# Layer 3 attention: four heads' outputs on quarters of the columns, softmax sums by GpSimd and a product with ones

## The chip, the cores and the metric

The kernel runs on one core of one Trainium2 chip. The metric is the device time of one execution in microseconds (us), smaller is better. All arithmetic is in float32. The engines are TensorE (PE in the profile; PEld is its weight load), VectorE (DVE), ScalarE (ACT), GpSimd (POOL) and SyncE (SP, which here only issues DMAs). Each works through its own list of instructions in order.

## What is computed

The whole network has four layers: a selective scan over an image, a deformable convolution, a linear-attention transformer with a mixture of experts, and a causal attention with a second mixture of experts. The change is in the attention of layer 3. It works on 4 images of 2304 tokens and 128 channels, with 4 heads of 32 channels:

```python
qkv = jnp.einsum('btc,oc->bto', x, qkv_w) + qkv_b
q, k, v = (heads(t) for t in jnp.split(qkv, 3, axis=-1))
att = jnp.einsum('bhqd,bhkd->bhqk', q, k) * scale
att = jnp.where(causal, att, -jnp.inf)
att = jax.nn.softmax(att, axis=-1)
out = jnp.einsum('bhqk,bhkd->bhqd', att, v)
return jnp.einsum('btc,oc->bto', out, out_w) + out_b
```

`x` is the layer-normed token array, and the result is added to the tokens. The experts of layer 3 follow.

## The kernel before

The function `_layer3` holds the attention. An image is cut into 6 blocks of 384 queries (`BLK`), numbered `j` = 0 to 5, and into 18 key tiles of 128 (`NT`). Block `j` needs its first 3(j+1) key tiles, since the attention is causal. The heads are taken as two pairs (`p` = 0, 1), two heads `r` in a pair. A unit is one key tile `t` of one pair of one block: 4 x 2 x 63 = 504 units in all.

A unit has two halves. `scores` forms, with one product per head on 64 of the rows each, the transposed scores in `scT` (128 keys x 2 heads x 384 queries, two PSUM banks, one buffer), lets ScalarE take exp of them into `pT` in SBUF (five buffers), and on the three key tiles of the diagonal lets GpSimd zero what is masked (`affine_select`). In the last two of these tiles only 256 or 128 queries are computed. `weighed` multiplies `pT` with the values and adds up over the key tiles in the PSUM bank `out`, three units later (`UNIT_LAG`). The tile `values` holds, next to a head's 32 value channels, 32 columns of ones, so that a head's product has 64 columns: 32 outputs and 32 copies of the softmax sum. Two heads fill 128 columns. At the end of a pair ScalarE copies `out` to `raw`, and four DMAs on SP's queue sort the outputs of the four heads into one tile and the sums into another. `divide` inverts the sums in two pieces (`invert`, VectorE), multiplies, and `output` projects the result and adds it to the tokens `T`.

For a stable softmax each query's maximum is subtracted. `largest` works it out one block ahead: `part` forms the scores of 128 queries against up to 512 keys in `sc` (four PSUM banks, one buffer), VectorE adds the causal mask on a row's last part (`later`) and reduces to the maxima (`mx`, `top`), whose negatives go into `spread`. At the end of a block `take` transposes `spread` (TensorE) and adds it into `q` (VectorE), for either pair. There are 5, 7, 9, 12 and 14 parts for blocks 1 to 5, and 3 for block 0.

`prepare` makes `q`, `k` and `v` of a block: `norm` (VectorE, `xn`), `turn` (GpSimd adds the output bias to `T`; TensorE transposes), four projections and `value`. `normed` computes mean and variance of an image (VectorE), and GpSimd a power of it. The transposes, projections, `take` and `output` share one PSUM bank (`ps`, one buffer).

The order on every engine is written out by hand (`manual_schedule`). For each block and pair the main loop runs over its key tiles: `scores`, then parts of the next block's maxima at an even pace, then one step of `divide` if any waits (two empty steps come first, and one between `invert` and `output`), then in every second unit one step of the preparation of the next image (`others`), then `weighed` of the unit three back.

Of the kernel before, what the change touches and what calls it, by code (L numbers as in the profile page):

```python
# [15 lines left out]
F32 = mybir.dt.float32  # L16
# [1892 lines left out]


KW = 512
UNIT_LAG = 3


def _layer3(ctx, env, io, T):

# [63 lines left out]
    def prepare(im, j):  # L1980

        at = bass.ts(j, BLK)
        t = {}

        def norm():
            t["xn"] = sp.tile([P, G3, C], F32, name="xn")
            for g in range(G3):
                i = j * G3 + g
                nc.vector.tensor_scalar(
                    t["xn"][:, g, :],  # L1990
                    im.T[:, i, :],
                    im.mv[:, i, 0:1],
                    im.rstd[:, i : i + 1],
                    op0=ALU.subtract,
                    op1=ALU.mult,
                )

        def turn():

            own = im.T[:, j * G3 : (j + 1) * G3, :]  # L2000
            nc.gpsimd.tensor_add(own, own, bias.to_broadcast([P, G3, C]))
            pt = psum(P, BLK)
            for g in range(G3):
                nc.tensor.transpose(pt[:, bass.ts(g, P)], t["xn"][:, g, :], ident)
            t["xT"] = sp.tile([P, BLK], F32, name="xT")
            nc.scalar.copy(t["xT"], pt)

        def project(s, p):
            pq = psum(P, BLK)
            nc.tensor.matmul(pq, w_qk[:, s, p, :], t["xT"], start=True, stop=True)  # L2010
            if s:
                nc.scalar.activation(
                    im.k[:, p, at], pq, AF.Identity, bias=b_qk[:, s, p : p + 1]
                )
            else:
                nc.vector.tensor_scalar(
                    im.q[:, p, at],
                    pq,
                    b_qk[:, s, p : p + 1],
                    DH3**-0.5,  # L2020
                    op0=ALU.add,
                    op1=ALU.mult,
                )

        def value():
            pv = psum(P, G3, C)
            for g in range(G3):
                nc.tensor.matmul(
                    pv[:, g, :], t["xT"][:, bass.ts(g, P)], w_v, start=True, stop=True
                )  # L2030
            nc.scalar.copy(
                im.v[:, j * G3 : (j + 1) * G3, :, :DH3],
                pv.rearrange("p g (h d) -> p g h d", d=DH3),
            )
# [63 lines left out]
    class Block:  # L2098


        def __init__(self, im, j, p):
            self.im, self.j, self.p = im, j, p
            self.last = (j + 1) * G3 - 1

    def scores(x, t):
        g0 = max(t - x.j * G3, 0)
        cols = slice(g0 * P, BLK)
        sc = pb.tile([P, 2, 512], F32, name="scT")
        for r in range(2):
            rows = slice(r * 64, r * 64 + 64)  # L2110
            nc.tensor.matmul(  # L2111
                sc[:, r, cols],
                x.im.k[rows, x.p, bass.ts(t, P)],
                x.im.q[rows, x.p, x.j * BLK + g0 * P : (x.j + 1) * BLK],
                start=True,
                stop=True,
            )
        pT = sp.tile([P, 2, BLK], F32, name="pT", bufs=UNIT_LAG + 2)
        nc.scalar.activation(pT[:, :, cols], sc[:, :, cols], AF.Exp)  # L2119
        if t >= x.j * G3:  # L2120
            own = pT[:, :, g0 * P : (g0 + 1) * P]
            nc.gpsimd.affine_select(
                out=own,
                in_=own,
                pattern=[[0, 2], [1, P]],
                compare_op=ALU.is_ge,
                fill=0.0,
                base=0,
                channel_multiplier=-1,
            )  # L2130
        x.__dict__.setdefault("pT", {})[t] = pT

    def weighed(x, t):
        g0 = max(t - x.j * G3, 0)
        cols = slice(g0 * P, BLK)
        if t == 0:
            x.out = po.tile([P, BLK], F32, name="out")
        pT = x.pT.pop(t)
        for r in range(2):
            nc.tensor.matmul(  # L2140
                x.out[r * 64 : r * 64 + 64, cols],
                x.im.v[:, t, 2 * x.p + r, :],
                pT[:, r, cols],
                start=t == 0,
                stop=t == x.last,
            )
        if t == x.last:

            raw = sp.tile([P, BLK], F32, name="raw")
            nc.scalar.copy(raw, x.out)  # L2150
            if x.p == 0:
                x.im.sums = [sp.tile([P, BLK], F32, name=f"sums{i}") for i in range(2)]
            for r in range(2):
                for i in range(2):
                    ch, at = (2 * x.p + r) * DH3, r * 64 + i * DH3
# [4 lines left out]
    def divide(x):  # L2160
        oT, den = x.im.sums

        def invert(i):
            part = bass.ts(i, BLK // 2)
            nc.vector.reciprocal(den[:, part], den[:, part])
            if i:
                nc.vector.tensor_mul(oT, oT, den)

        wait = lambda: None
        return [  # L2170
            wait,
            wait,
            lambda: invert(0),
            lambda: invert(1),
            wait,
            output(x.im, x.j, oT),
        ]

    for s in spread:
        nc.gpsimd.memset(s, 0.0)  # L2180
    for v in values:
        nc.gpsimd.memset(v, 1.0)
    images = [Image(b) for b in range(NB)]
    blocks = [Block(im, j, p) for im in images for j in range(NBLK) for p in range(NP3)]

    def preparation(im):
        return normed(im) + [s for j in range(NBLK) for s in prepare(im, j)]

    def run(steps):
        for s in steps:  # L2190
            s()

    with tc.manual_schedule(engines=ORDERED):
# [10 lines left out]
        waiting, done, doing = [], [], []  # L2204
        for i, x in enumerate(blocks):
            n = x.last + 1
            if x.j == 0 and x.p == 0 and x.im.b + 1 < NB:
                others += preparation(images[x.im.b + 1])
            following = blocks[i + NP3] if i + NP3 < len(blocks) else None
            if x.p == 0:  # L2210
                parts, take = largest(following.im, following.j) if following else ([], None)
                total, units = len(parts), 0
                if following and following.im is x.im and x.im.b == 0:

                    need = (NBLK - 1 - following.j) * (2 + 2 * NP3 + 1)
                    need += 0 if x.im.b + 1 == NB else len(preparation(images[1]))
                    while len(others) > need:
                        others.pop(0)()
            for t in range(n):
                scores(x, t)  # L2220
                units += 1
                while parts and (total - len(parts)) * (NP3 * n - 1) < total * units:
                    parts.pop(0)()
                if doing:
                    doing.pop(0)()
                if others and (t % 2 == 0 or n < 7):
                    others.pop(0)()
# [6 lines left out]
            if x.p == NP3 - 1:  # L2234
                run(parts)
                if following and following.im is not x.im:
                    run(others)
                    others = []
                if take:
                    take()  # L2240
        for y, s in waiting:
            weighed(y, s)
            if s == y.last and y.p == NP3 - 1:
                doing += divide(y)
        run(doing)

# [158 lines left out]
```

## Time and profile before

| | us |
|---|---|
| median of 3 runs | 12411.82 |
| lowest and highest run | 12407.96, 12424.98 |
| the profiled execution | 12295.53 |
| its span, first to last instruction | 12293.8 |
| layer 3: first `sc` product to last addition to `T` | 10797.5 to 12090.1 |

| engine | busy in the span |
|---|---|
| TensorE | 10700.3 (87%) |
| weight loads | 8228.4 (67%) |
| VectorE | 8434.0 (69%) |
| ScalarE | 6893.9 (56%) |
| GpSimd | 4463.2 (36%) |

The mean granted TensorE clock was 0.956 of full speed. Busy times are averages over four unlike layers, so a change in layer 3 has to be read in layer 3's stretch of the trace. The profiled execution was 116.3 us shorter than the median of the timed ones. A matmul's recorded end is modelled, and the weight loads of TensorE overlap its products, so starts are surer than durations. A float32 product appears as two MATMUL and two LDWEIGHTS records.

### The profile page before, as it was taken

What the parts mean: (1) busy time and instruction counts of PE and PEld (TensorE: products, weight loads), DVE (VectorE), ACT (ScalarE), POOL (GpSimd) and SP (SyncE); (2) the same over time, 40 slices, a digit from 0 to 9 for tenths busy, and PEclk for the clock granted to TensorE, in tenths of its full rate; (3) what the DMA queues carried; (4) which work ended last, traced back from release to release, by engine and by line L of the source; (5) the groups of instructions that cost most, each with busy time, mean ns of one, the idle gap of its engine ahead of it and who ended that gap; (6) DMA issues with size and microseconds to landing.
All of it is one profiled execution on the core that took longest, in us unless ns stands there. A gap on an engine that the chain in (4) does not pass through costs nothing.

```text
span 12293.8 us, 192110 instructions
## 1 busy us (share of the span) xinstructions
PE 10700.3 (87%) x71008; PEld 8228.4 (67%) x71008; DVE 8434.0 (69%) x15140; ACT 6893.9 (56%) x13190; POOL 4463.2 (36%) x4799
## 2 busy tenths in 40 slices
PE   7778788977888787789979999999999999689997
PEld 6667666766676666578857777777777777433333
DVE  6998889888888889755455655655665665455553
ACT  5777777777777777611135555655565565323332
POOL 2443334333333434377733333333333333110001
PEclk9999999999999999999979999999999999889998
DMA  3221222222212222266600000000000000300003
GB/s 123 69 71 64 76 80 69 65 75 83 67 66 72 69 80 68 80 182 198 195 31 2 4 2 4 5 2 4 2 4 3 3 1 1 126 8 8 8 9 129
DMA packets 329875, 677.47 MB, mean 55 GB/s; under 512 B 41556, under 2 KB 152168, under 8 KB 328048
## 3 DMA queue, kind: packets, MB, share of 16 engines
q1 hardware_dynamic: 276064, 493.50, 12.6%
q0 software_dynamic: 51840, 169.91, 4.9%
q8 instruction: 569, 9.32, 0.3%
q14 instruction: 362, 2.97, 0.1%
q10 hardware_dynamic: 1040, 1.77, 0.0%
HBM read 602.63 MB, written 71.85 MB: 55 GB/s over the span
## 4 chain that ended last, share of the span: by engine, by line
PE 37%; DVE 6%; ACT 4%; DMA 3%; POOL 3%; issue 3%; SPq 0%; ACTq 0%; DVEq 0%; POOLq 0%
PE psum L1466 4%; PE psum L1458 4%; PE pc L1352 3%; PE psum L1402 3%; PE scT L2111 3%; PE psum L1372 2%; POOL g L990 2%; PE psum L1212 2%; DMA g<-table,idx 2%; PE psum L1213 2%; PE psum L1146 2%; PE out L2140 2%; PE sc L2055 2%; PE psum L1290 1%; ACT pT L2119 1%
## 5 line engine op out<-in xcount | busy, mean ns | idle before, releaser
L576 ACT ACTIVATE hs<-ps,bct 128x256 f32<-128x256 f32 x4608 | 1857.5, 475 | 1172.6 <-PE ps L570 1122.1
L570 PE MATMUL ps<-ident,h 128*128 128x128 f32 x9216 | 1492.4, 294 | 786.5 <-DVE h L556 612.3
L570 PEld LDWEIGHTS ps<-ident,h 128*128 128x128 f32 x9216 | 1080.4, 148 | 1170.8 <-DVE h L556 719.5
L584 PE MATMUL yp<-ident,hs 128*128 128x128 f32 x9216 | 1400.4, 288 | 28.6 <-ACT ys L599 28.6
L516 ACT ACTIVATE dA<-delta,l_Al 128x768 f32<-128x768 f32 x1536 | 1388.3, 936 | 0.3
L523 POOL TENSOR_TENSOR h<-du,rB 128x512 f32<-128x512 f32 x768 | 1079.4, 1405 | 766.0 <-PE ps L570 689.5
L584 PEld LDWEIGHTS yp<-ident,hs 128*128 128x128 f32 x9216 | 1154.2, 150 | 82.7 <-ACT ys L599 57.7
L556 DVE TENSOR_TENSOR_SCAN h<-dA,h 128x256 f32<-128x256 f32 (+1 forms) x1024 | 1082.6, 1057 | 27.2
L556 DVE TENSOR_TENSOR_SCAN h<-dA,carry,h 128x768 f32<-128x768 f32 x512 | 1028.7, 2009 | 10.6 <-ACT dA L516 10.6
L1206 POOL TENSOR_TENSOR T<-T,bias 128x384 f32<-128x384 f32 x384 | 384.1, 1000 | 1560.5 <-DVE fn L1134 1520.3
L498 POOL TENSOR_SCALAR_AFFINE_SELECT dB<-bct 128x512 f32<-128x512 f32 x768 | 750.4, 977 | 355.4 <-PE b L530 238.7
L556 DVE TENSOR_TENSOR_SCAN h<-dA,carry,b 128x512 f32<-128x512 f32 x512 | 645.4, 1261 | 267.3 <-PE b L530 247.9
L530 PE MATMUL b<-dB,duT 128*128 128x128 f32 x6144 | 826.9, 278 | 0.8 <-ACT duT L456 0.8
L990 POOL DMA_INDIRECT g<-table,idx x648 | 705.1, 1088 | 242.1 <-issue 139.7
L2119 ACT ACTIVATE pT<-scT 128x768 f32<-128x768 f32 (+2 forms) x504 | 378.1, 750 | 724.9 <-PE scT L2111 724.9
L530 PEld LDWEIGHTS b<-dB,duT 128*128 128x128 f32 x6144 | 766.6, 196 | 2.4 <-POOL h L523 1.2
L1003 PE MATMUL pt<-ident,gw 128*128 128x128 f32 x5184 | 661.7, 283 | 98.9 <-DVE gw L997 94.7
L563 POOL COPY carry<-h 128x2 f32<-128x2 f32 x512 | 97.8, 191 | 1780.9 <-DVE h L556 1722.4
L997 DVE TENSOR_TENSOR gw<-g,wq 128x512 f32<-128x512 f32 x648 | 446.0, 694 | 422.8 <-DMA g<-table,idx 366.0
L1003 PEld LDWEIGHTS pt<-ident,gw 128*128 128x128 f32 x5184 | 608.7, 193 | 146.8 <-DVE gw L997 113.4
L527 DVE TENSOR_TENSOR h<-du,rB 128x512 f32<-128x512 f32 x768 | 628.2, 818 | 2.7 <-DMA rB<-rows 2.5
L1219 ACT ACTIVATE wksq<-psum,l_cols 128x384 f32<-128x384 f32 x192 | 111.6, 581 | 788.3 <-DVE wk L1217 788.3
(394 smaller groups left out, 22793.0 us busy)
## 6 DMA issues: line engine op xcount, KB each, us to landing
rB<-rows SPq DMA_DIRECT2D x768, 384.0 KB, 3.4
w<-f_w SPq DMA_DIRECT2D x64, 1024.0 KB, 12.1
table<-zero SPq DMA_DIRECT2D x162, 128.0 KB, 1.9
table<-tok SPq DMA_DIRECT2D x16, 1152.0 KB, 9.7
g<-table,idx POOLq DMA_INDIRECT x648, 3.8
yd<-y SPq DMA_DIRECT2D x4, 2304.0 KB
sums<-raw SPq DMA_DIRECT2D x192, 48.0 KB, 2.0
xb<-x SPq DMA_DIRECT2D x42, 192.0 KB, 3.4
```

Of the source, the lines that this page charges most:

```text
L498: nc.gpsimd.affine_select(out=x.dB[n], in_=x.bc[:, m0 : m0 + CT // P, n : n + 1].to_broadcast([P, CT // P, P]), pattern=[[0, CT // P], [1, ...
L516: nc.scalar.activation(dA, x.delta[:, d, :], AF.Exp, scale=A[:, d, x.k, n : n + 1])
L523: nc.gpsimd.tensor_mul(h[:, 1, own], x.du[:, 1, own], x.rB[n][:, own])
L527: nc.vector.tensor_mul(x.h[n][:, :, own], x.du[:, :, own], b)
L530: nc.tensor.matmul(b0[:, bass.ts(m, P)], x.duT[:, m, :], x.dB[n][:, m, :], start=True, stop=True,)
L556: nc.vector.tensor_tensor_scan(h, da, b, initial=first, op0=ALU.mult, op1=ALU.add)
L570: nc.tensor.transpose(tt[:, m, bass.ts(d, P)], x.h[n][:, d, bass.ts(2 * q + m, P)], ident)
L576: nc.scalar.activation(hs, tt[:, m, :], AF.Copy, scale=x.bc[:, 2 * q + m, NS + n : NS + n + 1])
L584: nc.tensor.matmul(yp[:, q, (2 * d + m) * P : (2 * d + m + 1) * P], hs[:, bass.ts(d, P)], ident, is_transpose=True, start=n == 0 and m == ...
L990: nc.gpsimd.indirect_dma_start(out=g, out_offset=None, in_=table, in_offset=bass.IndirectOffsetOnAxis(ap=idx[:, j : j + 1], axis=0),)
L1003: nc.tensor.matmul(pt[:, t - t0, :], gw[:, q, :], ident, start=q == 0, stop=q == 3)
L2119: nc.scalar.activation(pT[:, :, cols], sc[:, :, cols], AF.Exp)
```

## The change

A block is no longer split into pairs. A step of the loop is one key tile for both pairs: `scores` of pair 0, `weighed` of the key tile two back (`UNIT_LAG` 2), `scores` of pair 1, then parts, two steps of `divide` and one of `others`. `values` loses its ones, and `weighed` now issues four products, each of a head's 32 value columns on a quarter of the array's columns, into `out`. The softmax sums are made in another way: for each unit GpSimd adds `pT` into a tile `sums` (a copy on the first key tile), and at the end of a block four products with a tile of ones add `sums` over the partitions (the step `sums` of `divide`), which ScalarE copies to `den`. The copy to `raw` becomes one to `oT`, and the DMAs go away. There are eight `pT` buffers. The cut marks leave out lines that stay the same.

```diff
-UNIT_LAG = 3
+UNIT_LAG = 2
...
-    values = [cp.tile([P, NT, NH3, 2 * DH3], F32, name=f"v{i}") for i in range(2)]
+    values = [cp.tile([P, NT, C], F32, name=f"v{i}") for i in range(2)]
+    ones = cp.tile([P, DH3], F32, name="ones")
...
-        pT = sp.tile([P, 2, BLK], F32, name="pT", bufs=UNIT_LAG + 2)
+        pT = sp.tile([P, 2, BLK], F32, name="pT", bufs=2 * (UNIT_LAG + 2))
...
+        if t == 0 and p == 0:
+            x.sums = sp.tile([P, NP3, 2, BLK], F32, name="sums")
+        total = x.sums[:, p, :, cols]
+        if t == 0:
+            nc.gpsimd.tensor_copy(total, pT[:, :, cols])
+        else:
+            nc.gpsimd.tensor_add(total, total, pT[:, :, cols])
+        x.pT[t, p] = pT
 
     def weighed(x, t):
...
-        pT = x.pT.pop(t)
-        for r in range(2):
-            nc.tensor.matmul(
-                x.out[r * 64 : r * 64 + 64, cols],
-                x.im.v[:, t, 2 * x.p + r, :],
-                pT[:, r, cols],
-                start=t == 0,
-                stop=t == x.last,
-            )
+        for p in range(NP3):
+            pT = x.pT.pop((t, p))
+            for r in range(2):
+                ch = slice((2 * p + r) * DH3, (2 * p + r + 1) * DH3)
+                nc.tensor.matmul(
+                    x.out[ch, cols],
+                    x.im.v[:, t, ch],
+                    pT[:, r, cols],
+                    start=t == 0,
+                    stop=t == x.last,
+                )
         if t == x.last:
-            raw = sp.tile([P, BLK], F32, name="raw")
-            nc.scalar.copy(raw, x.out)
...
-                    nc.sync.dma_start(
-                        x.im.sums[i][ch : ch + DH3, :], raw[at : at + DH3, :]
+            x.oT = sp.tile([P, BLK], F32, name="oT")
+            nc.scalar.copy(x.oT, x.out)
+
+    def divide(x):
+        t = {}
+        def sums():
+            pd = psum(P, BLK)
+            for p in range(NP3):
+                for r in range(2):
+                    h = 2 * p + r
+                    nc.tensor.matmul(
+                        pd[h * DH3 : (h + 1) * DH3, :],
+                        ones,
+                        x.sums[:, p, r, :],
+                        start=True,
+                        stop=True,
                     )
+            t["den"] = sp.tile([P, BLK], F32, name="den")
+            nc.scalar.copy(t["den"], pd)
...
         return [
             wait,
-            wait,
+            sums,
             lambda: invert(0),
             lambda: invert(1),
             wait,
-            output(x.im, x.j, oT),
+            output(x.im, x.j, x.oT),
         ]
...
             for t in range(n):
-                scores(x, t)
-                units += 1
-                while parts and (total - len(parts)) * (NP3 * n - 1) < total * units:
-                    parts.pop(0)()
-                if doing:
-                    doing.pop(0)()
-                if others and (t % 2 == 0 or n < 7):
-                    others.pop(0)()
-                waiting.append((x, t))
-                if len(waiting) > UNIT_LAG:
+                scores(x, t, 0)
+                if len(waiting) == UNIT_LAG:
                     y, s = waiting.pop(0)
                     weighed(y, s)
-                    if s == y.last and y.p == NP3 - 1:
+                    if s == y.last:
                         doing += divide(y)
+                elif doing:
+                    doing.pop(0)()
+                scores(x, t, 1)
+                waiting.append((x, t))
+                while parts and (total - len(parts)) * max(n - 1, 1) < total * (t + 1):
+                    parts.pop(0)()
+                for _ in range(2):
+                    if doing:
+                        doing.pop(0)()
+                if others:
+                    others.pop(0)()
```

More of the change, by code (lines that the diff above doesn't have):

```diff
@@ L2030, in value @@
                 )
-            nc.scalar.copy(
-                im.v[:, j * G3 : (j + 1) * G3, :, :DH3],
-                pv.rearrange("p g (h d) -> p g h d", d=DH3),
-            )
+            nc.scalar.copy(im.v[:, j * G3 : (j + 1) * G3, :], pv)
         return [norm, turn] + [
@@ L2098, in _layer3, with __init__, scores @@
     class Block:
-        def __init__(self, im, j, p):
-            self.im, self.j, self.p = im, j, p
+        def __init__(self, im, j):
+            self.im, self.j = im, j
             self.last = (j + 1) * G3 - 1
-    def scores(x, t):
+            self.pT = {}
+    def scores(x, t, p):
         g0 = max(t - x.j * G3, 0)
@@ L2112, in scores @@
                 sc[:, r, cols],
-                x.im.k[rows, x.p, bass.ts(t, P)],
-                x.im.q[rows, x.p, x.j * BLK + g0 * P : (x.j + 1) * BLK],
+                x.im.k[rows, p, bass.ts(t, P)],
+                x.im.q[rows, p, x.j * BLK + g0 * P : (x.j + 1) * BLK],
                 start=True,
@@ L2130, in scores @@
             )
-        x.__dict__.setdefault("pT", {})[t] = pT
+        if t == 0 and p == 0:
[6 more added lines that the diff above has]
+        x.pT[t, p] = pT
     def weighed(x, t):
@@ L2137, in weighed @@
             x.out = po.tile([P, BLK], F32, name="out")
-        pT = x.pT.pop(t)
-        for r in range(2):
-            nc.tensor.matmul(
-                x.out[r * 64 : r * 64 + 64, cols],
-                x.im.v[:, t, 2 * x.p + r, :],
-                pT[:, r, cols],
-                start=t == 0,
-                stop=t == x.last,
-            )
-        if t == x.last:
-            raw = sp.tile([P, BLK], F32, name="raw")
-            nc.scalar.copy(raw, x.out)
[L2151 to L2155, printed above, removed]
-                    nc.sync.dma_start(
-                        x.im.sums[i][ch : ch + DH3, :], raw[at : at + DH3, :]
-                    )
-    def divide(x):
-        oT, den = x.im.sums
+        for p in range(NP3):
[9 more added lines that the diff above has]
+                )
+        if t == x.last:
+            x.oT = sp.tile([P, BLK], F32, name="oT")
[13 more added lines that the diff above has]
+                        stop=True,
+                    )
+            t["den"] = sp.tile([P, BLK], F32, name="den")
+            nc.scalar.copy(t["den"], pd)
         def invert(i):
             part = bass.ts(i, BLK // 2)
-            nc.vector.reciprocal(den[:, part], den[:, part])
+            nc.vector.reciprocal(t["den"][:, part], t["den"][:, part])
             if i:
-                nc.vector.tensor_mul(oT, oT, den)
+                nc.vector.tensor_mul(x.oT, x.oT, t["den"])
         wait = lambda: None
@@ L2180, in _layer3 @@
         nc.gpsimd.memset(s, 0.0)
-    for v in values:
-        nc.gpsimd.memset(v, 1.0)
+    nc.gpsimd.memset(ones, 1.0)
     images = [Image(b) for b in range(NB)]
-    blocks = [Block(im, j, p) for im in images for j in range(NBLK) for p in range(NP3)]
+    blocks = [Block(im, j) for im in images for j in range(NBLK)]
     def preparation(im):
@@ L2206, in _layer3 @@
             n = x.last + 1
-            if x.j == 0 and x.p == 0 and x.im.b + 1 < NB:
+            if x.j == 0 and x.im.b + 1 < NB:
                 others += preparation(images[x.im.b + 1])
[L2209 to L2217, printed above, removed]
-                        others.pop(0)()
@@ L2219, in _layer3 @@
-            for t in range(n):
-                scores(x, t)
-                units += 1
-                while parts and (total - len(parts)) * (NP3 * n - 1) < total * units:
-                    parts.pop(0)()
-                if doing:
-                    doing.pop(0)()
-                if others and (t % 2 == 0 or n < 7):
-                    others.pop(0)()
-                waiting.append((x, t))
-                if len(waiting) > UNIT_LAG:
+            following = blocks[i + 1] if i + 1 < len(blocks) else None
@@ new lines, in _layer3 @@
+            parts, take = largest(following.im, following.j) if following else ([], None)
+            if following and following.im is x.im and x.im.b == 0:
+                need = (NBLK - 1 - following.j) * (2 + 2 * NP3 + 1)
+                need += 0 if x.im.b + 1 == NB else len(preparation(images[1]))
+                while len(others) > need:
+                    others.pop(0)()
+            total = len(parts)
+            for t in range(n):
+                scores(x, t, 0)
+                if len(waiting) == UNIT_LAG:
@@ L2230, in _layer3 @@
                     y, s = waiting.pop(0)
                     weighed(y, s)
-                    if s == y.last and y.p == NP3 - 1:
+                    if s == y.last:
                         doing += divide(y)
[L2234 to L2240, printed above, removed]
+                elif doing:
+                    doing.pop(0)()
@@ new lines, in _layer3 @@
+                scores(x, t, 1)
[6 more added lines that the diff above has]
+                if others:
+                    others.pop(0)()
+            run(parts)
+            if following and following.im is not x.im:
+                run(others)
+                others = []
@@ L2241, in _layer3 @@
+            if take:
+                take()
         for y, s in waiting:
             weighed(y, s)
-            if s == y.last and y.p == NP3 - 1:
+            if s == y.last:
                 doing += divide(y)
```

## The prediction

> **What bounds the kernel now.** I read the page first (layer 3 starts near slice 36, where TensorE shows 9 tenths), then the groups of its stretch by shape (10797 to 12095 us: busy us, mean ns, then idle before and releaser), then the timeline.
>
> ```profile
> L2111 PE MATMUL scT<-q,k 64*128 64x384 f32 x1632 | 379.0, 542 | 38.3 <-ACT pT L2119 38.1
> L2140 PE MATMUL out<-pT,v 128*64 128x384 f32 x1632 | 355.6, 515 | 0.0
> L2066 DVE TENSOR_REDUCE mx<-sc 128x4 f32<-128x2048 f32 x144 | 329.9, 2291 | 216.3 <-PE sc L2055 215.6
> L2001 POOL TENSOR_TENSOR T<-T,bias 128x384 f32<-128x384 f32 x23 | 23.0, 998 | 158.3 <-DVE xn L1989 158.3
> ```
>
> TensorE looks like the bound, and the products to be halved (`out`) are its second item. A unit with nothing else in it, in the timeline, tells more:
>
> ```profile
> 11416.02 0.92 PE L2111 MATMUL scT<-q,k 64*128 64x384 f32 x4 [0.17 <-ACT pT L2119]
> 11416.86 0.87 PE L2140 MATMUL out<-pT,v 128*64 128x384 f32 x4
> 11417.04 0.81 ACT L2119 ACTIVATE pT<-scT 128x768 f32<-128x768 f32 x1 [1.07 <-PE scT L2111]
> 11417.90 0.92 PE L2111 MATMUL scT<-q,k 64*128 64x384 f32 x4 [0.17 <-ACT pT L2119]
> ```
>
> The second scores start when exp releases `scT`, which has one buffer: this loop lasts 1.885 us whatever TensorE adds. From start to start the scores' slot is 0.84 and that of `out` 0.80. So `out` mostly fills a gap that is there anyway, and costs time only where other products push the slots beyond 1.885.
>
> **The change, part by part.** *Slots.* A step is now: scores, one `out` group of four heads, scores, everything else. The experts ahead of layer 3 show quarters of the columns side by side:
>
> ```profile
> 10756.16 1.08 PE L1806 MATMUL psum<-w,hT 128*32 128x128 f32 x32 [0.67 <-DVE hT L1800]
> ```
>
> These are 16 products in 1.08 us; in a row, at the 0.26 of a 128-column transpose here, they would take 4. So I take 0.80 for four heads. By start to start the other slots are: `sc` of 512 columns 1.07, a projection 0.80 to 0.86, the transposes 0.78, `output` 0.87, the new `sums` 0.85 (as `out`). A unit, or half step, lasts the longer of 1.885 and its slots. Bare: two units 3.77, a step 3.77, no gain. One `sc` per pair: 2.71 + 1.885 = 4.60 becomes 1.885 + 1.91 = 3.80. I laid the code's order of parts and products over this rule. Sums over the images by block index, before and after: 0: 55, 55; 1: 126, 106; 2: 173, 155; 3: 224, 201; 4: 281, 252; 5: 279, 273. That is 1138 and 1042: **-96**. (Block 4 of the last image: 65.4 and 56.3; the trace has 68.0.) From the first block to the last `out` the trace has 1270, so 132 are waits outside the rule, mostly in blocks 0 and 1, where VectorE's maxima bound.
>
> *New waits.* Replaying steps by hand:
> - Two parts in one step: the second waits for the first's reduction, 1.21 + 2.29 + 0.05 = 3.55 after its start against a slot of 1.07. In blocks 2 and 3 eight times 2.5, less 7 in similar places before: +13.
> - The step of `output`. Both halves of `invert` are now issued in the step ahead of it. From that step's second scores: reduction until 4.3, reciprocals 2 x 1.34, product 0.56, done at 7.6. TensorE reaches `output` at 5.7 to 6.6. The addition to T then queues behind the next reduction (until 10.0) and lasts 0.55, and the next user of the one `ps` bank, ready at 8.5, starts at 10.6. Before, this is seen in small:
>
> ```profile
> 11352.89 0.56 DVE L2167 TENSOR_TENSOR sums<-sums,sums 128x384 f32<-128x384 f32 x1
> ...
> 11354.03 0.94 PE L2092 MATMUL ps<-l_owT,sums 128*128 128x128 f32 x6 [0.56 <-DVE q L2016]
> 11356.09 0.54 DVE L2094 TENSOR_TENSOR T<-T,ps 128x384 f32<-128x384 f32 x1
> 11356.69 0.91 PE L2010 MATMUL ps<-xT,l_wqk 128*128 128x384 f32 x2 [1.72 <-DVE T L2094]
> ```
>
>  TensorE works in order, so the next scores stand behind these waits, and exp and GpSimd behind the scores. Net +2 in each of blocks 1 to 4: +32.
> - A product behind `sums` waits about 0.65 for the copy of `den`, 14 times: +9. Block 1 keeps 10 of the rule's 20, as VectorE's 30 us there stay: +10. Twelve products of image 0 run in a row through `ps`, at about 1.7 instead of 0.85: +10.
> - The last step hides some of the way to `take`, 20 x 0.5, and at the end four DMAs (3.8 from first issue to landing) give way to `sums` and a copy: -12. The other 188 DMAs and SP's queue hide behind units; taking them off gains nothing, nor does the memset of `values` (GpSimd is done at 10777.5, the mean and variance it next needs come at 10781.2).
>
> On ACT 48 copies of `raw` become 24 of `oT` and 24 of `den`, 0.48 each, in its idle 1.07 a unit: 0, and +23 if that cover were gone. Together **+62**.
>
> *GpSimd.* 384 columns take 998 ns, 512 take 1277 (median of L523), 2304 take 5039: 768 take 1.81, 512 1.27, 256 0.73, a copy of 768 about 0.95. That is 360 x 1.81 + 48 x 1.27 + 48 x 0.73 + 48 x 0.95 = 793, with 59 of masks and 37 of the rest 890 us of 1270. A unit of 1.885 covers an add of 1.81 and eight `pT` buffers lend slack, so the adds themselves cost 0. With L523's mean (1405 for 512, 2.74 ns an element) an add takes 2.1 and bare stretches pay: up to +24. Behind the adds queue the masks (needed two tiles later), the bias addition and the power of `rstd` (3.2 us); the slack covers these.
>
> *The port.* Small VectorE instructions have stood still until GpSimd's ended:
>
> ```profile
> 11888.00 0.41 POOL L2122 TENSOR_SCALAR_AFFINE_SELECT pT<-pT 128x256 f32<-128x256 f32 x1 [0.63 <-ACT pT L2119]
> 11888.03 0.47 DVE L2072 TENSOR_SCALAR spread<-top 128x2 f32<-128x2 f32 x2
> ```
>
> The pair takes 0.24 otherwise. In layer 2 a `fn` of 0.34 took 4.09 beside a 5.04 us add. "GPSIMD Engine Reference" of the Trainium skill, section Specifications, has the rule: GpSimd shares its SBUF interfaces with VectorE, in contention with instructions in a 2-port mode or with two SBUF inputs. By the trace the reciprocals are exempt (1.34 beside a bias addition too); if every SBUF-only instruction paid, they would add 24 x 2 x 0.77 = 37. With GpSimd 85% busy (1.81 to a mean unit of some 2.15) the mean wait is 0.85 x 1.81 / 2 = 0.77. On the path lie the product before `output` and the last `spread` before `take`: 2 x 0.77 x 20 blocks = **+31**. If the three `xn` and both of a `spread` pair wait for an add each, +90; if nothing waits, 0.
>
> *The clock.* Granted clock is the number ahead of the last two:
>
> ```profile
> 11478.00:11482.00 4.00, 2.19 (x16) 0.64 (x12) 3.83 (x10) 0.60 (x1) 0.41 (x1) 0.92 0.01 2
> 11482.00:11486.00 4.00, 3.39 (x24) 1.61 (x20) 3.68 (x10) 0.38 (x1) 0.41 (x1) 0.50 0.00 0
> 11486.00:11490.00 4.00, 4.00 (x18) 1.18 (x16) 2.82 (x13) 1.29 (x2) 0.41 (x1) 0.50 0.16 40
> ```
>
> A gap of 1.8 us at 11479 halved it for some 8 us. The skill's "TensorE: Matmul & The Clock Gate", Part 1, asks for an idle window of about 3.4 us; by that my gaps of 1.9 to 3.2 would cost 0. By the trace some do (here), some don't (11354: 1.00 throughout). I take 45% of 30 new gaps (16 at `output`, 14 at second parts) at 2.5 each: **+34**, bounds 0 and 75.
>
> Sum: -96 + 62 + 31 + 34 = **+31** on the profiled execution's 12295.5. The median shown, 12411.8, is 116.3 above that execution; I carry the difference over: **12443**. The median's 0.2%, some 25 us, is about what a measurement of this kernel can tell from no change.
>
> **The rivals.**
> 1. *The slots win* (not slower). Place: the filled steps of blocks 1 to 4; price -96 plus what waits remain. For: TensorE 9 tenths busy. It decides as long as new waits stay below 96 / 20 = 4.8 us a block; mine are 6.3. With half of my 127, -32; with a quarter, -64: 12348 to 12380. Chance 0.18.
> 2. *A draw*: the port and the clock cost nothing, -96 + 62 = -34, or one of them does, about 0. Takes in my own sum's lower end: 12387 to 12436. Chance 0.27.
> 3. *GpSimd becomes the bound or blocks VectorE at every small instruction*: +31 + 24, or 62 + 90 + 34 - 96 = +90: 12467 to 12502. For: an add fills 96% of a bare unit. Against: 890 of 1270. Chance 0.14.
> 4. *The quarters don't run side by side*: `out` 1.6 a step, 252 x (0.8 - 0.24) = +140 on top: 12580. Against: L1806. Chance 0.02.
>
> **How the numbers follow.** The forecast, moderately slower, has 0.39; with rivals 3 and 4, slower by over 0.2% has 0.55, the draw 0.27, faster 0.18. The range goes from half of rival 1's gain (-91 at its best, cut at -60) to rival 3 with both prices at once (+115): 12352 to 12527; the forecast alone 12437 to 12460.
>
> **What would show it.** Bare units stay at 1.89. L2140's busy time falls by about 190 while the stretch from `spread` to the last `out` does not shrink. L2092 shows waits of 1 to 3 us on DVE in blocks 1 to 4, and the product behind it on T. POOL is 65 to 75% busy, an add at 1.8 us. L2072 and L1989 rise to about 0.5 to 1 us. The clock has dips behind `output`. Wrong: idle of L2092's kind under 1 us and a layer shorter by 60; or adds above 2.1.

## The result, and the profile after

The changed kernel takes 12551.16 us (median of 4 runs, 12539.69 to 12569.39), the kernel before in the same comparison 12413.85 (12407.96 to 12424.98): a ratio of 1.0111, interval 1.0093 to 1.0128. It is slower by 137 us. The prediction had +31, and +115 with both of its prices at their highest. The direction was right, the size was not.

The two profiled executions differ by 244 us of span, but 107 of that lie outside the attention, in layers 0 to 2 ahead of it, which the change does not touch. Such amounts are seen between chips: the kernel before took 12296 us (median) on one chip of the experiments and 12400, 12412 and 12423 on three others, so each ratio below is to the kernel before on the same chip. What follows is measured in layer 3 alone: from the start of the first addition of the causal mask to the start of the last addition to `T`, called the stretch. It is 1291.2 us before (10798.4 to 12089.6) and 1428.4 after (10906.5 to 12334.9), **+137.2**, which agrees with the medians. The busy time of the engines in the stretch, before and then after (the number behind POOL's is the granted TensorE clock, then DMA share and GB/s):

```profile
core 0: us, PE busy (x) PEld busy (x) DVE busy (x) ACT busy (x) POOL busy (x), PEclk, DMA share, GB/s
10798.40:12089.60 1291.20, 1158.16 (x6303) 408.82 (x6303) 650.69 (x858) 446.74 (x645) 91.28 (x171) 0.97 0.03 8
```

```profile
10906.50:12334.90 1428.40, 1097.24 (x6495) 382.83 (x6495) 730.99 (x858) 447.59 (x645) 872.96 (x675) 0.88 0.00 1
```

TensorE works 61 us less and the layer lasts 137 longer. VectorE has 80 us more, although it does the same instructions (858 in both), and the clock falls from 0.97 to 0.88. Groups of the stretch by shape (busy us, mean ns, then idle before and its releaser), first three of VectorE in the kernel before, then the changed kernel:

```profile
L1989 DVE TENSOR_SCALAR xn<-T,mv,rstd 128x128 f32<-128x128 f32 x69 | 20.0, 346 | 1.2 <-POOL rstd L1976 1.2
L2072 DVE TENSOR_SCALAR spread<-top 128x2 f32<-128x2 f32 x144 | 17.7, 169 | 2.5
L2167 DVE TENSOR_TENSOR sums<-sums,sums 128x384 f32<-128x384 f32 x24 | 13.4, 558 | 0.8
```

```profile
L2137 POOL TENSOR_TENSOR sums<-sums,pT 128x768 f32<-128x768 f32 x360 | 651.0, 1809 | 267.5 <-ACT pT L2118 246.7 <-POOL sums L2137 0.4
L2110 PE MATMUL scT<-q,k 64*128 64x384 f32 x1632 | 410.8, 583 | 82.2 <-ACT pT L2118 80.3
L2150 PE MATMUL out<-pT,v 128*32 128x384 f32 x1632 | 188.3, 536 | 0.0
L1990 DVE TENSOR_SCALAR xn<-T,mv,rstd 128x128 f32<-128x128 f32 x69 | 58.5, 901 | 4.7 <-POOL rstd L1977 4.7
L2070 DVE TENSOR_SCALAR spread<-top 128x2 f32<-128x2 f32 x144 | 45.5, 361 | 2.5
L2184 DVE TENSOR_TENSOR oT<-oT,den 128x384 f32<-128x384 f32 x24 | 30.1, 1254 | 0.8
```

`out` falls from 355.6 to 188.3, by 167 where the prediction named about 190. The add on GpSimd takes 1809 ns (1.81 was forecast). `scT` is no more work than before, but its busy time rises from 379.0 to 410.8: the lower clock. The last three are small instructions of VectorE with operands in SBUF (`oT<-oT,den` is the product before `output`). They take 83 us more than before, which is all of VectorE's 80. A bare step in the timeline is as predicted:

```profile
12286.00 0.92 PE L2110 MATMUL scT<-q,k 64*128 64x384 f32 x4 [0.97 <-ACT pT L2118]
12286.85 0.85 PE L2150 MATMUL out<-pT,v 128*32 128x384 f32 x8
12287.89 0.92 PE L2110 MATMUL scT<-q,k 64*128 64x384 f32 x4 [0.19 <-ACT pT L2118]
12289.77 0.30 PEld L2110 LDWEIGHTS scT<-q,k 64*128 64x128 f32 x4 [1.58 <-ACT pT L2118]
```

Eight records of `out`, four heads, take 0.85: the quarters run side by side. The step is 3.77, twice 1.885. So the time is not lost where nothing else is done. It is lost in places like the step of `output`, here in the second image's block 4:

```profile
11540.19 2.56 DVE L2182 RECIPROCAL den<-den 128x192 f32<-128x192 f32 x2
...
11542.78 1.98 DVE L2184 TENSOR_TENSOR oT<-oT,den 128x384 f32<-128x384 f32 x1
...
11544.82 0.94 PE L2090 MATMUL ps<-l_owT,oT 128*128 128x128 f32 x6 [2.26 <-DVE oT L2184]
11545.40 2.29 DVE L2064 TENSOR_REDUCE mx<-sc 128x4 f32<-128x2048 f32 x1
11548.08 0.55 DVE L2092 TENSOR_TENSOR T<-T,ps 128x384 f32<-128x384 f32 x1
11548.68 1.65 PE L2029 MATMUL ps<-l_wv,xT 128*128 128x128 f32 x6 [2.93 <-DVE T L2092]
11550.26 1.65 PE L2110 MATMUL scT<-q,k 64*128 64x384 f32 x4
11551.84 1.51 PE L2150 MATMUL out<-pT,v 128*32 128x384 f32 x8
```

This is the replay of the prediction: `output` waits 2.26 for the product, the addition to `T` stands behind the next reduction, the next user of `ps` waits 2.93 for it. Two things differ from the replay: the product itself takes 1.98 instead of 0.56, and after the two gaps the scores take 1.65 instead of 0.92 and `out` 1.51 instead of 0.85, which is half clock.

Where TensorE stood waiting for VectorE, over the whole stretch (the waits of PE: total us, times, longest), before and after:

```profile
PE sc L2055 <- DVE mx L2066: 25.0, 27, 2.6
...
PE ps L2010 <- DVE T L2094: 12.2, 10, 1.7
PE ps L2092 <- DVE sums L2167: 8.4, 2, 7.5
...
PE ps L2004 <- DVE xn L1989: 4.4, 4, 1.2
```

```profile
PE sc L2053 <- DVE mx L2064: 81.8, 39, 3.2
PE ps L2005 <- DVE xn L1990: 30.4, 24, 2.8
...
PE ps L2090 <- DVE oT L2184: 28.3, 13, 3.9
PE ps L2029 <- DVE T L2092: 8.9, 4, 2.9
PE ps L2011 <- DVE T L2092: 8.5, 5, 2.9
```

Three rows have grown: the wait for `sc` to be reduced (+57), for `xn` (+26) and for `oT` (+20; before, the product wrote into `sums`). The waits for the addition to `T` have hardly grown: 18 us in three rows before, 22 after. Summed over all products, TensorE waits for VectorE 89 us before and 220 after.

### The profile page after: what moved, and what is told of

Same layout as the page of the kernel before. It is cut to its first block, busy times and chain, and to the rows that moved or that the text cites. A ratio compares the mean times of both kernels' runs of the same rounds, so it can differ in the third digit from the quotient of the medians.

```text
span 12538.0 us, 192809 instructions
## 1 busy us (share of the span) xinstructions
PE 10665.7 (85%) x71200; PEld 8249.3 (66%) x71200; DVE 8502.9 (68%) x15140; ACT 6888.9 (55%) x13190; POOL 5184.4 (41%) x5302
## 3 DMA queue, kind: packets, MB, share of 16 engines
q10 hardware_dynamic: 1040, 1.77, 0.0%
## 4 chain that ended last, share of the span: by engine, by line
PE 39%; DVE 8%; ACT 4%; POOL 2%; issue 2%; another core or an unknown queue 1%; DMA 1%; SPq 0%; ACTq 0%; DVEq 0%; POOLq 0%
PE psum L1466 4%; PE psum L1458 4%; PE pt L1003 4%; PE pc L1352 3%; PE psum L1402 3%; PE scT L2110 2%; PE psum L1372 2%; PE psum L1212 2%; PE psum L1213 2%; PE psum L1146 2%; DVE mx L2064 1%; PE psum L1290 1%; PE sc L2053 1%; ACT pT L2118 1%; POOL sums L2137 1%
## 5 line engine op out<-in xcount | busy, mean ns | idle before, releaser
L2137 POOL TENSOR_TENSOR sums<-sums,pT 128x768 f32<-128x768 f32 (+2 forms) x456 | 746.5, 1638 | 275.5 <-ACT pT L2118 246.7
L990 POOL DMA_INDIRECT g<-table,idx x648 | 663.4, 1024 | 397.3 <-DVE gw L997 189.4
L1003 PEld LDWEIGHTS pt<-ident,gw 128*128 128x128 f32 x5184 | 653.0, 208 | 179.6 <-DVE gw L997 119.8
```

The costliest lines, as they stand in the source:

```text
L990: nc.gpsimd.indirect_dma_start(out=g, out_offset=None, in_=table, in_offset=bass.IndirectOffsetOnAxis(ap=idx[:, j : j + 1], axis=0),)
L1003: nc.tensor.matmul(pt[:, t - t0, :], gw[:, q, :], ident, start=q == 0, stop=q == 3)
L2137: nc.gpsimd.tensor_add(total, total, pT[:, :, cols])
```

## The experiments

Four causes were to be told apart: the halved `out` products bring less than the 96 forecast; GpSimd's adds hold VectorE up; the new order makes TensorE wait; the clock falls. The table has the stretch, from one profile each, and the ratio to the kernel before, from runs on the same chip. Stretch and ratio say the same within some 15 us, so differences of that size between stretches are not taken as shown.

| kernel | stretch, us | clock in it | PE waiting for DVE, us | ratio, interval |
|---|---|---|---|---|
| before | 1291.2 | 0.97 | 89 | 1 |
| changed | 1428.4 | 0.88 | 220 | 1.0111 (1.0093 to 1.0128) |
| e_noadd | 1368.6 | 0.88 | 175 | 1.0065 (1.0048 to 1.0082) |
| e_old_adds | 1348.2 | 0.94 | 115 | 1.0045 (1.0030 to 1.0059) |
| e_warm | 1391.5 | 0.95 | 130 | 1.0083 (1.0067 to 1.0100) |
| e_even | 1315.3 | 0.92 | 149 | 1.0019 (1.0011 to 1.0027) |
| e_even_noadd | 1266.4 | 0.92 | 112 | 0.9967 (0.9955 to 0.9978) |
| e_parts | 1356.8 | 0.91 | 180 | 1.0061 (1.0040 to 1.0082) |
| e_div | 1409.9 | 0.88 | 199 | 1.0099 (1.0078 to 1.0120) |
| e_free | 1374.5 | 0.88 | 165 | 1.0069 (1.0044 to 1.0094) |
| e_xn | 1404.6 | 0.87 | 183 | 1.0092 (1.0077 to 1.0108) |
| e_even_free | 1248.3 | 0.95 | 108 | 0.9970 (0.9960 to 0.9980) |
| e_before_free | 1285.0 | 0.96 | 81 | 0.9998 (0.9989 to 1.0006) |
| e_half | 1239.5 | 0.95 | 112 | 0.9961 (0.9948 to 0.9973) |

**The adds left out (e_noadd).**

```diff
         if t == 0:
             nc.gpsimd.tensor_copy(total, pT[:, :, cols])
-        else:
-            nc.gpsimd.tensor_add(total, total, pT[:, :, cols])
```

> The changed kernel, but GpSimd only copies the weights of the first key tile into `sums`; the 456 adds of the later tiles are left out, so the divisors lack their share. Instructions of the other engines and their order stay. Layer 3's stretch (first mask addition to last addition to T) is 1428 in the changed kernel and 1291 in the one before. Theory 1 (gaps at TensorE halve its clock; the adds matter little): the gaps at `output` and at second parts stay, so does the clock at about 0.88: 1390 to 1430, total 12510 to 12550. Theory 2 (VectorE stands still behind the adds): VectorE's small instructions return to 0.35 (`xn`), 0.17 (`spread`) and 0.56 us (product before `output`), 84 us of VectorE are saved, and the stretch falls to about 1320, total about 12440. Theory 3 (the new order makes TensorE wait for VectorE's reductions whatever GpSimd does): as theory 1, with the clock as a consequence.

Measured: 1368.6, 60 of the 137 gone. VectorE's small instructions are back at their old durations, the clock stays at 0.88:

```profile
L1990 DVE TENSOR_SCALAR xn<-T,mv,rstd 128x128 f32<-128x128 f32 x69 | 20.6, 354 | 4.8 <-POOL rstd L1977 4.8
L2070 DVE TENSOR_SCALAR spread<-top 128x2 f32<-128x2 f32 x144 | 17.8, 169 | 2.5
L2182 DVE TENSOR_TENSOR oT<-oT,den 128x384 f32<-128x384 f32 x24 | 13.5, 564 | 0.8
```

No theory has it alone: 60 belong to the adds, and 77 remain with no add in the kernel.

**The adds put into the kernel before (e_old_adds).** The cut marks leave out the number of `pT` buffers, which goes from five to eight.

```diff
...
+        if t == 0:
+            x.gsum = sp.tile([P, 2, BLK], F32, name="gsum")
+        total = x.gsum[:, :, cols]
+        if t == 0:
+            nc.gpsimd.tensor_copy(total, pT[:, :, cols])
+        else:
+            nc.gpsimd.tensor_add(total, total, pT[:, :, cols])
```

> The kernel before, with GpSimd's copies and adds of `pT` put in, into a tile that nobody reads (8 `pT` buffers, as in the changed kernel). Order, products and divisors are those of before. Theory 2 (VectorE stands still behind the adds): the stretch of 1291 grows by most of the 137, to about 1380 (total 12500), and `xn`, `spread` and small products lengthen as in the changed kernel. Theories 1 and 3 (the gaps come from the new order of products, reciprocals and `output`): about 1300 to 1315, total 12420 to 12440, and the clock in the stretch stays at about 0.96.

Measured: 1348.2, +57 (52 by the medians), between the two expectations. Within the noise this is the price in the other order too (60, or 57 by the medians). What lengthens:

```profile
L2119 ACT ACTIVATE pT<-scT 128x768 f32<-128x768 f32 x408 | 330.6, 810 | 626.6 <-PE scT L2111 618.0 <-POOL gsum L2137 3.5 <-POOL T L2001 2.9
L1989 DVE TENSOR_SCALAR xn<-T,mv,rstd 128x128 f32<-128x128 f32 x69 | 47.5, 742 | 1.2 <-POOL rstd L1976 1.2
L2072 DVE TENSOR_SCALAR spread<-top 128x2 f32<-128x2 f32 x144 | 37.0, 302 | 2.5
```

Exp hardly waits for GpSimd (3.5 and 2.9 us in this shape), so it is not late `pT` buffers. VectorE is busy for 61 us more (711.7 to 650.7), and the stretch is 57 longer. TensorE's own waits for VectorE grew by only 26 of these; its clock fell too, from 0.97 to 0.94, and how much of the 57 that is was not tried.

**The clock kept up (e_warm).** `warm(x, n)`, whose definition is cut here, issues n pairs of score products that nobody reads.

```diff
...
+                first = True
                 while parts and (total - len(parts)) * max(n - 1, 1) < total * (t + 1):
+                    if not first:
+                        warm(x, 3)
+                    first = False
                     parts.pop(0)()
                 for _ in range(2):
                     if doing:
+                        last = len(doing) % 6 == 1
+                        if last:
+                            warm(x, 2)
                         doing.pop(0)()
+                        if last and others:
+                            warm(x, 2)
```

> The changed kernel with extra products that nobody reads (score products of key tile 0 into a `scT` tile) put into the places where TensorE waits: three pairs between two `sc` groups of one step, two pairs ahead of `output`, two behind it. They take TensorE time only where it would wait, but for some 0.5 us a place. Theory 1 (clock): the dips behind `output` and second parts go, the clock of the stretch rises from 0.88 to about 0.95, and the stretch falls from 1428 to about 1370, total about 12490. Theories 2 and 3 (the waits themselves cost the time, the clock is a by-product that hides behind exp and VectorE): 1430 to 1450, total 12550 to 12575.

Measured: 1391.5 at a clock of 0.95, 37 us less than the changed kernel (39 by the medians). This is what the higher clock brings less what the extra products cost. So the fall of the clock costs some 37 or more; how much more, this run does not say.

**The work spread out (e_even).**

```diff
+            def due(units):
+                while parts and (total - len(parts)) * (2 * n - 1) < total * units:
+                    parts.pop(0)()
...
                 scores(x, t, 0)
+                due(2 * t + 1)
...
-                while parts and (total - len(parts)) * max(n - 1, 1) < total * (t + 1):
-                    parts.pop(0)()
+                due(2 * t + 2)
+                if others:
+                    others.pop(0)()
                 for _ in range(2):
                     if doing:
                         doing.pop(0)()
-                if others:
-                    others.pop(0)()
...
             lambda: invert(0),
+            wait,
             lambda: invert(1),
             wait,
+            wait,
             output(x.im, x.j, x.oT),
```

> The changed kernel with its other work spread out: `sc` parts are due at half steps (after the first scores too), a step of another image's preparation goes ahead of the division's steps, and the two halves of the reciprocal, and `output`, lie a step apart, as they did before the change. No instruction is added or removed. Theory 3 (second parts in one step, and `output` behind two reciprocals in a row): the waits shorten, the clock rises to 0.93 or more, the stretch falls to 1320 to 1350, total 12440 to 12470. Theory 2 (VectorE stands still behind the adds): only some 30 of the 137 go, 1400, total 12520. Theory 1 goes with theory 3 here.

Measured: 1315.3, 113 of the 137 gone, more than theory 3 asked for, at a clock of 0.92 where it asked for 0.93, with the adds still there and `xn` still at 913 ns. No instruction was taken away, only places were changed.

**Both (e_even_noadd).** The edits of e_even and e_noadd together.

> The spread-out order of the other work and, as well, GpSimd's adds of the later key tiles left out (the divisors lack their share). If the adds and the order are two separate prices, as their single runs say (60 for the adds, 113 for the order, of a stretch of 1428), both together give about 1255 to 1275, total 12235 to 12260, below the kernel before: the halved `out` products are then worth some 20 to 35 and not the 96 of the slots. If the spread order only made room for VectorE's waiting (theory 2), leaving the adds out brings little more: 1305 to 1315, total 12310.

Measured: 1266.4, as the two separate prices say (49 below e_even). Against the kernel before, this is what halving `out` brings when neither the adds nor the once-a-step order eat it: 25 us in this profile, 40 by the medians (interval 27 to 56). The profiled execution was the slowest of the seven, so 25 is likely too little.

**Which part of the order (e_parts, e_div).** The first takes only the two `due` edits of e_even, the second only the three empty steps of the division.

> The changed kernel (stretch 1428, total about 12432 on the chip of the earlier experiments) with one edit: `sc` parts are due at half steps, so two stand in a row less often; the division's list stays. Theory A (second parts in one step are the larger price, blocks 2 and 3 grew by 33 and 35 over four images): 1350 to 1365, total 12355 to 12370. Theory B (`output` behind two reciprocals in a row is): 1395 to 1415, total 12400 to 12420. The prediction had 13 for the first and 32 for the second.

> The changed kernel with one edit: the two halves of the reciprocal, and `output`, lie about a step apart; `sc` parts stay due once a step. Theory A (second parts in a row): 1400 to 1415, total 12405 to 12420. Theory B (`output`): 1350 to 1370, total 12355 to 12375.

Measured: 1356.8 and 1409.9, that is 72 and 19 saved (64 and 14 by the medians; the 14 is within their noise): theory A. The pacing of the parts is the larger price. In e_parts the wait for `mx` fell by 21 us, all waits for VectorE by 40, and the time at half clock from 347 to 248 us (the clock was only ever full or half here, so that time is twice the lost share of the stretch). In e_div the wait for `oT` is still there (27.0 us for 28.3); blocks 0, 2, 3 and 4 became 33 us shorter and block 1 15 longer. The two together make 91 of e_even's 113; the rest is its third edit or their joint effect, which was not tried apart.

**VectorE freed from the adds (e_free).**

```diff
-                top = sp.tile([P, 2, NP3], F32, name="top")
-                nc.vector.reduce_max(top, t["mx"][:, :, :, : s + 1], axis=AX.X)
                 for p in range(NP3):
                     neg = spread[p][:, i - j * G3, (1 - p) * DH3 :: 2 * DH3]
-                    nc.vector.tensor_scalar_mul(neg, top[:, :, p], -1.0)
+                    nc.vector.reduce_max(
+                        neg, t["mx"][:, :, p, : s + 1], axis=AX.X, negate=True
+                    )
...
+                im.shift = sp.tile([P, NT], F32, name="shift")
+                nc.gpsimd.tensor_tensor(im.shift, im.mv[:, :, 0], im.rstd, ALU.mult)
+                nc.gpsimd.tensor_scalar_mul(im.shift, im.shift, -1.0)
...
+                nc.scalar.activation(
+                    t["xn"][:, g, :],
+                    im.T[:, i, :],
+                    AF.Identity,
+                    bias=im.shift[:, i : i + 1],
+                    scale=im.rstd[:, i : i + 1],
+                )
```

> The changed kernel with `spread` written by a negating maximum (two reductions for one reduction and two products) and `xn` made on ScalarE, so that of the small VectorE instructions only the product before `output` still waits for GpSimd's adds; the adds stay. Theory P (the adds' price of 60 is VectorE standing still): about 67 us of VectorE's 80 go, and the stretch falls by 35 to 55, to about 1385, total 12375 to 12400. Theory Q (the price is GpSimd's queue: `pT` buffers come free late, 27.6 us of exp's idle time): no more than 15, about 1415 to 1430, total 12420 to 12435.

Measured: 1374.5, 54 saved: theory P. GpSimd does all its adds (875.96 us busy), exp still waits 23.1 for them in its main shape (27.6 in the changed kernel), and 54 of the adds' 60 are gone (48 of 57 by the medians). The negating maxima are not held up:

```profile
L2070 DVE TENSOR_REDUCE spread<-mx 128x2 f32<-128x8 f32 x32 | 3.7, 159 | 0.5
L2186 DVE TENSOR_TENSOR oT<-oT,den 128x384 f32<-128x384 f32 x24 | 24.6, 1025 | 0.8
```

The product before `output`, which this edit leaves alone, still is (1025 ns).

**The control (e_before_free).** The same edit in the kernel before, without adds.

> A control: the kernel before, with `spread` by negating maxima and `xn` on ScalarE; no adds on GpSimd. Theory P (the 54 us that this edit took in the changed kernel were VectorE standing still behind adds): here it takes only the 20 us of `xn` off VectorE, gives them to ScalarE, and the stretch stays within 10 of 1291. The other theory (VectorE's load bounds both kernels): 20 to 40 less, ratio 0.997 to 0.998.

Measured: a ratio of 0.9998 and 6 us in the stretch. In the old order the lighter load of VectorE is worth next to nothing, so what the edit gained in the changed kernel was, in the main, the standing still. Whether the load counts in the new order, without adds, was not tried.

**One of the two (e_xn).** Only `xn` goes to ScalarE.

> The changed kernel with only `xn` moved to ScalarE; `spread` still waits for the adds. In the changed kernel `xn` costs VectorE 38 us more than before, `spread` 28, the product before `output` 17. The prediction put the last two on the path and left `xn` out: then this saves about 0 to 10 of the 54. If every wait of VectorE's small instructions counts where its maxima are in line behind them, it saves 25 to 35: total about 0.002 of the time below the changed kernel, a ratio of 1.008 to 1.009.

Measured: 1404.6, 24 saved, by the medians 28 (+109 us over the kernel before in place of +137). The rest of e_free's 54, some 30, is `spread`, by difference. The step of the prediction that left `xn` out, and all but the last `spread`, does not hold.

**Both repairs (e_even_free).** The edits of e_even and e_free; nothing is left out.

> The changed kernel with both repairs: the spread-out order, and `spread` by negating maxima and `xn` on ScalarE. Nothing is left out. Alone they took 113 and 54 from the stretch of 1428. If they are separate prices, 1260 to 1280 remain, under the 1291 of the kernel before: 0.998 to 0.999 of its time. If they overlap (both take away the same waits for VectorE), 1290 to 1310 remain, 1.000 to 1.001.

Measured: 1248.3, 12375.97 us to 12412.30, a ratio of 0.9970 (0.9960 to 0.9980). This version beats both kernels. It saves about the two separate prices (180 to 113 + 54, or by the medians 174 to 115 + 48).

**Only the halving (e_half).**

```diff
-        for r in range(2):
+        for r in range(0 if t % 2 and t != x.last else 2):
```

> The kernel before, with the `out` products of every second key tile left out (so the outputs and divisors lack those tiles); everything else, its order too, stays. It asks what halving `out` can bring by itself, with no new order, no adds and no new wait. By the prediction's rule (a half step lasts the longer of 1.885 and its slots) the sum of the slots falls from 1138 to 1057: the stretch of 1291 would become 1210, the ratio 0.9935. If the slots that exceed 1.885 end on VectorE's maxima or on the projections' bank instead, as the 25 us of the spread-out order without adds say: 1255 to 1275, ratio 0.997 to 0.999.

Measured: 1239.5, -52 to the rule's -81; neither expectation was met. By block index 0 to 5 over the images (from end to end of `take`) the rule saves 4, 12, 14, 18, 22 and 11; measured were 1, 1, 7, 13, 18 and 12. The rule holds for the late blocks and fails in blocks 1 and 2. What it left out is seen in the trace: TensorE waits 112 us for VectorE (89 before), 11 of the growth for `mx`, and spends 131 us at half clock (87 before). With less work TensorE lost some of its own clock; by half of the 44 us, an estimate, that took up to 22 of the missing 29.

## Why the prediction was right or wrong, point by point

- *Bare steps do not gain, the quarters run side by side.* Right: 3.77 and 0.85. Rival 4 falls.
- *Slots, -96.* This is the term that failed most, by its size. In the old order the halving itself brought 52 of the 81 that the same rule gives (e_half); in the spread-out order without adds it brought 25, or 40 by the medians. Of the 106 us between the forecast and the result, 44 to 71 lie here. The rule let a half step last the longer of the exp loop and TensorE's slots. It had no place for what TensorE then waits for VectorE (`sc` product, reduction, next `sc` product), but for ten us in block 1, nor for the clock that TensorE loses by having less to do.
- *The port, +31.* Right mechanism, half the size, and the second term that failed: 60 by leaving the adds out, 57 by putting them into the old order. An instruction waited less than the 0.77 assumed, which took GpSimd to be busy for 85% of the time, where it was for 61%: 0.70 for the product before `output`, 0.56 for `xn`, 0.19 for `spread`. But more of them count. The term had two a block on the path. `xn` (24 to 28 us) and the other `spread` instructions count as well: TensorE's transposes wait for `xn` (30.4 us, 4.4 before), and in VectorE's list a reduction stands behind the `spread` of the part before it. The prediction wrote this down as its upper bound (+90) and did not take it. Reciprocals were exempt, as it said (1318 ns).
- *Two parts in one step, +13.* Counted wrong. I had eight of them, those in blocks 2 and 3 (and 14 in the term of the clock). The code has 28: 12 in block 0, 8, 4 and 4 in blocks 1 to 3. The wait of `sc` on its reduction grew by 57, and pacing the parts at half steps took away 72. Part of the 72 is clock (0.88 to 0.91), and 18 of it lie in block 4, which has no second parts: there the even pace must help in another way, perhaps by keeping the reductions clear of VectorE's other work. My rule gives the two paces the same slots, so it could not show this.
- *The step of `output`, +32.* The timeline shows the mechanism, and the rows named (1 to 3 us on VectorE, then on `T`) appear. But the wait for `oT` grew by 20 and that for `T` by some 4, and spreading the division alone took 19 away (not clear of the noise) without shortening the wait for `oT`. The term was too high, and what e_div saved is not explained.
- *The clock, +34.* Some 37 or more by e_warm, so the term was not too large. The count behind it was wrong. It had 30 new gaps, of which 45% count, so 13 or 14 new falls of the clock. By the clock's records the stretch had 10 falls before and 48 after, and 87 us at half clock before and 347 after. That is clock time worth 130 us, but part of it falls where TensorE had slack. How the order's price divides between waits and clock stays open.
- *GpSimd's adds, 0.* Duration right (1.81), load 61% where 65 to 75% was named. Exp waited 27.6 us in its main shape for buffers that adds held; e_free shows that most of the price is not there.
- *Two slips in the text of the prediction.* The draw's first case, -34, is 12378 and lies below the range given for the draw. The fall of the clock shown at 11482 lasted 10.24 us by the clock's records, not some 8.

Two experiments make a chain from the kernel before to the changed one. By the stretch, halving `out` (e_even_noadd) is -25, order and clock (from there to e_noadd) +102, the adds +60, which is 137; by the medians the chain is -40, +120 and +57. The prediction had -96, +96 and +31. Its sum for new waits and clock came near by luck: the second parts cost several times what they were given, the step of `output` less. The gain was taken two to four times too large, and the port half as large as it is. Of the rivals, the third (GpSimd blocks VectorE at every small instruction) named what the term of the port left out, but by itself it ended at 12502.

## What to carry to other kernels

Work taken off an engine pays only where that engine closes the loop: before counting it as saved, lay every loop through its buffers (here product, reduction, next product) over the steps, and count each place where two users of one buffer meet. When steady GpSimd work is added beside VectorE, give each small VectorE instruction of a kind that is held up (here a product or a subtraction with all tensors in SBUF, but no reduction and no reciprocal) a wait for it, not only the one that looks last. Keep what an engine waits for a step away from where it is needed: moving places, with no instruction taken out, was worth 113 us here. And work taken off TensorE can lower its clock: see whether what is left still fills it.

## What the runs showed of the hardware

A gap of 1.70 us was enough to halve TensorE's clock; scores then took 1.65 us instead of 0.92 (changed kernel):

```profile
12134.55 0.48 PE L2075 MATMUL ps<-ident,spread 128*128 128x128 f32 x1 [1.70 <-DVE spread L2070]
12135.67 0.90 PE L2075 MATMUL ps<-ident,spread 128*128 128x128 f32 x3 [0.65 <-DVE q L2077]
12136.50 1.65 PE L2110 MATMUL scT<-q,k 64*128 64x384 f32 x4
```

Yet the gap of 1.72 that the prediction shows at 11354, in the kernel before, left the clock at 1.00. The clock's own records tell why. In all fourteen profiles the granted clock of the stretch is 1.00 or 0.50, and it changes only on a grid of 3.41 us. Here are slices of that grid, each with TensorE's busy time and its clock, first the changed kernel around the lines above, then the kernel before:

```profile
12130.98:12134.39 3.41, 1.87 (x18) 1.00 0.00 0
12134.39:12137.80 3.41, 2.61 (x8) 0.50 0.00 0
12137.80:12141.22 3.41, 3.41 (x18) 0.50 0.00 0
12141.22:12144.63 3.41, 0.99 (x12) 1.00 0.00 0
12144.63:12148.04 3.41, 3.41 (x16) 0.50 0.00 0
```

```profile
11351.63:11355.05 3.41, 2.77 (x18) 1.00 0.00 0
11355.05:11358.46 3.41, 1.77 (x8) 1.00 0.00 0
11358.46:11361.87 3.41, 3.24 (x20) 1.00 0.00 0
```

How busy a slice is tells the clock of the next. Over the fourteen stretches, 244 slices at full clock had TensorE busy for less than 45% of their time, and half clock followed every one; 3939 had it busy for 65% or more, and half clock followed none. In between both happened (141 of 393), as in the rows of 1.87 and 1.77. At half clock, all 431 slices that were busy for less than 85% were followed by another, and of 363 that were busy for 97% or more only 13 were. (Busy times rest on modelled ends.) So the length of a gap alone does not tell its price; what counts is how full it leaves its slice. The prediction set an idle window of about 3.4 us, from the Trainium skill's "TensorE: Matmul & The Clock Gate", Part 1, against its own row. The length is what these records show; the window need not be idle.

VectorE's instructions differ in whether they wait for GpSimd's, and writing the same two numbers in another way decides it: as a product of a `top` already in SBUF, 128x2, 361 ns beside the adds and 169 without them; as a negating maximum into the same strided places, 152 to 161 ns beside the adds.
